# Another order of the x products of a step, and of VectorE's first operations, in a one-core LSTM

## The chip, the cores and the metric

The kernel runs on one core of a Trainium2 chip. The metric is device time in microseconds from launch to end. The engines are named as in the profile: PE (TensorE, matmul; PEld its weight loads), DVE (VectorE), ACT (ScalarE), POOL (GpSimd) and SP (SyncE, which here only issues DMAs). Each engine runs its own queue in order; they meet through semaphores.

## The reference

An LSTM over 512 steps, batch 32, width 512, four gates, whose outputs are added to its input:

```
xW = einsum('ntd,dg->ntg', x, Wx) + b          # x: 32 x 512 x 512, Wx: 512 x 2048
def step((h, c), xw_t):
    a = xw_t + h @ Wh                          # Wh: 512 x 2048
    i, f, o = sigmoid(a[:, :512]), sigmoid(a[:, 512:1024]), sigmoid(a[:, 1024:1536])
    g = tanh(a[:, 1536:])
    c = f * c + i * g
    h = o * tanh(c)
    return (h, c), h
out = x + h over all steps                     # h starts as cond_1024, c as 0; float32
```

## The kernel before

**Two kinds of matmul share PE.** The h part (`h_part`, L667 to L678) of step k is h times Wh, 64 matmul instructions that add into PSUM banks which ACT has seeded with the x part (`seed_first`, `seed_last`). It needs the transposed h of the step before (`ht`, L706). The x part, x times Wx plus bias, depends on no h; it is worked out ahead, in pieces which stand on PE between the h part of one step and that of the next, while the cell (`cell`: ACT L694 to L696 and L700, DVE L697 to L706) turns gates into the next h.

**The x part by fewer products.** The first four steps, the next four and the last sixteen are multiplied directly (`direct`, L604; L620 adds the bias). All others go through two layers of sums. The outer layer takes 24 steps of x (three rows of eight; a "block" below) by 20 products of sums of x blocks ("nodes", DVE L348) with sums of Wx blocks; each of the 20 is a *job*. The inner layer takes a job by seven products, numbered 1 to 7, from four "x sums" of the node (DVE L376 to L379) and differences of the weights (DVE L211 to L213, tiles t; factors made of several blocks are made once by `push_factors`, stored in DRAM, and reloaded for each job into the rings wa and wb). Steps 8 to 39 (the head) use the inner layer alone, two factors for each product; this is also where the first jobs lie.

**The windows of a job.** A job has a window w; window v goes with step k = v - 4. `products(v)` (L422 to L429) issues, from several jobs at once: product 1 of job v, product 6 of job v - 1, product 7 of job v - 2, products 2 and 3 of job v - 3, product 4 of job v - 4; product 5 in the job's own window or the next. Five of six windows start a job. Products 1, 6 and 7 add up in one half of a bank `acc`; 5 goes into `p5` (p in the trace), 2, 3 and 4 into two of three banks `pp`. A job's half of `acc` shares its bank with the half of the job two windows away.

**What is read in between.** `evacuate(v)` (L431 to L459), issued before `products(v)`, reads the running products: first, by a call with `FIRST_SUMS` as its room, due x sums and nodes; then `finish`, which reads the complete halves of `pp` (DVE L563 adds, ACT L551 copies); ACT's copy of `acc` after product 1 (L442) and of `p5` (L446); DVE's L449, acc plus p5 after product 6, ahead of product 7; more due sums (room `BETWEEN`); ACT L455 and L456, which seed the job's `pp`; and DVE's L457, acc plus p5 after product 7.

**What DVE does when.** `due` is a list sorted by window: x sums, nodes, sums of finished products (L579), factor sums. `run_due(v, room)` goes through it from the front. What is due by v is done; what is due later is done if it is ready and its columns plus 160 fit into the room left. An x sum is charged 128 + 160 = 288, a node 512 + 160 = 672, an L579 1024 + 160 = 1184. When the first call has done something, the whole of `FIRST_SUMS` is charged to the step's room of 3400.

**POOL and SP.** POOL adds the residual (L710) after each transposed h and the bias to the loaded x part (L652). SP issues, step by step, the loads of the x part (L649), of the rings (wa L771, wb L775) and of the rows, and the stores. Reloading a buffer of the ring wa waits for the last product that reads it, 6 or 5.

**The start** (L789 to L832) is written out by hand. On PE: 16 direct pieces into four banks, `products(0)`, then the direct parts of the steps 4 to 7, into the gate banks again, with `products(1)` to `products(3)` between them. On DVE: `t_sums(i)`, three differences each (L211 to L213), for the eight weight blocks; the first x sums (`prepare(0)`, L280 to L283, which need a loaded row); `keep_direct` (L620), which empties the four banks; then the factor sums (L248, L252).

Of the kernel before, what the change touches and what calls it, by code (L numbers as in the profile page):

```python
# [44 lines left out]
NODES = 8  # L45
FIXED = 160
ROOM = 3400
FIRST_SUMS = 600
BETWEEN = 1200
HEAD_ROOM = 5000  # L50
SLACK = [1, 1, 3]
# [55 lines left out]
def windows_of(k):  # L107

    return [k + 4]
# [17 lines left out]
def kernel(  # L127
# [49 lines left out]
    def load_residual(t):  # L177
        m = xr[t] = xr[t + 1] = opool.tile([P, 2, NJ, B], F32, name=f"xr_{t}", tag="xr")
        i, a = divmod(t, ROW)
        nc.sync.dma_start(  # L180
            out=m.rearrange("p t q b -> p (t q b)"),
            in_=x[i][:, a * P : (a + 2) * P],
        )
# [24 lines left out]
    def t_sums(i):  # L208
        w, t = raw[i], tt_[i]
        return [  # L210
            lambda: nc.vector.tensor_sub(t[:, 0:2], w[:, 1::2], w[:, 0:2]),  # L211
            lambda: nc.vector.tensor_sub(t[:, 2], w[:, 3], t[:, 0]),
            lambda: nc.vector.tensor_sub(t[:, 3], w[:, 2], t[:, 2]),  # L213
        ]
# [85 lines left out]
    def run_due(v, room):  # L300

        i = 0
        while i < len(due):
            window, _, columns, fn, ready = due[i]
            if window > v and (columns + FIXED > room or not ready(v)):
                i += 1
                continue
            assert ready(window)
            due.pop(i)
            fn()  # L310
            room -= columns + FIXED
            i = 0
# [88 lines left out]
    def product(job, s):  # L401
        dst = {
            1: job.acc,
            6: job.acc,
            7: job.acc,
            5: p5[:, 0],
            2: job.pp[0][:, 0],
            3: job.pp[0][:, 1],
            4: job.pp[1][:, 0],
        }[s]  # L410
        for m, (a, w) in enumerate(job.factors(s)):
            for t in range(4):
                nc.tensor.matmul(  # L413
                    dst[t * B : (t + 1) * B],
                    a[:, t],
                    w,
                    start=s in (1, 5) and m == 0,
                    stop=True,
                    skip_group_check=True,
                )  # L420

    def products(v):  # L422
        for late, ss in ((1, (6,)), (4, (4,)), (2, (7,)), (0, (1,)), (0, (5,)), (1, (5,)), (3, (2, 3))):
            job = jobs.get(v - late)
            for s in ss if job else ():
                if s != 5 or job.w5 == v:
                    product(job, s)
                if s == 4:
                    job.release()  # L429

    def evacuate(v, room):  # L431
        before = len(due)
        run_due(v - 0.5, FIRST_SUMS)
        taken = FIRST_SUMS if len(due) < before else 0
        for half, late in ((1, 5), (0, 4)):
# [160 lines left out]
    def flat(bank):  # L596
        return bank if len(bank.shape) == 2 else bank.rearrange("p n c -> p (n c)")

    def direct(t, bank, qs=range(4)):
        i, a = divmod(t, ROW)  # L600
        for q in qs:
            k, e = divmod(q, 2)
            for j in range(NJ):
                nc.tensor.matmul(  # L604
                    flat(bank)[j * B : (j + 1) * B],
                    rows[i][:, a, q],
                    raw[NJ * k + j][:, 2 * e : 2 * e + 2].rearrange("p n c -> p (n c)"),
                    start=q == 0,
                    stop=True,
                    skip_group_check=True,  # L610
                )

    def keep_direct(t, bank, room=None):
        if room is not None:
            xw[t] = room
        elif t < 4:
            xw[t] = upool.tile([P, G * P], F32, name=f"xw_{t}", tag="xw", bufs=4)
        else:
            xw[t] = node_free[t - 4].rearrange("p t e b -> p (t e b)")
        nc.vector.tensor_add(xw[t], flat(bank), bias_sb)  # L620
# [25 lines left out]
    def load_xw(t):  # L646
        xw[t] = upool.tile([P, G * P], F32, name=f"xw_{t}", tag="xw", bufs=4)
        i, a = divmod(t, ROW)
        nc.sync.dma_start(out=xw[t], in_=stored[i][a])  # L649

    def add_bias(t):
        nc.gpsimd.tensor_add(xw[t], xw[t], bias_sb)  # L652
# [3 lines left out]
    def seed_first(t):  # L656
        if t < T:
            nc.scalar.copy(gates[t % 2][:, 0:IFG], xw[t][:, 0:IFG])  # L658

    def seed_last(t):  # L660
        if t < T:
            nc.scalar.copy(gates[(t + 1) % 2][:, IFG:], xw[t][:, IFG:])
# [66 lines left out]
    def prepare(v):  # L729

        job = jobs.get(v)
        ops = []
        if job is None or job.w >= START:
            return ops
        i, j = job.kind
        for k in range(2):
            if (i, k) not in head_sums:
                if (i, 0) not in head_sums:
                    both = spool.tile([P, 2, 4, 4, B], F32, name=f"s_h{i}", tag="sums", bufs=2)
                head_sums[i, k], more = inner_sums(block(raw_block(i, k)), both[:, k])  # L740
                ops += more
        job.factors = lambda s: [
            (left(block(raw_block(i, k)), s, head_sums[i, k]), raw_factor(NJ * k + j, s)) for k in range(2)
        ]
        job.finish = finish_unit(job, i, j)
        job.release = lambda: None
        return ops
# [40 lines left out]
    with tc.manual_schedule():  # L788
        warm = work.tile([P, G, P], F32, name="warm", tag="s")  # L789
        nc.scalar.activation(warm[:, 0], c_init, AF.Sigmoid)  # L790
        for m in range(3 * NJ):
            nc.tensor.matmul(
                pps[2][m % NJ * B : (m % NJ + 1) * B].rearrange("p n c -> p (n c)"),
                c_init[:, 0:B],
                c_init.unsqueeze(1).to_broadcast([P, 4, P]),
                start=True,
                stop=True,
            )
        nc.vector.transpose(
            bias_sb.rearrange("p (m l) -> p m l", l=B),  # L800
            bias_t.unsqueeze(2).to_broadcast([P, G * NJ, B]),
        )
        firsts = [gates[0], gates[1], pps[0], pps[1]]
        for q in range(4):
            for t in range(4):
                direct(t, firsts[t], (q,))
        for i in range(5):
            for op in t_sums(i):
                op()
        for op in prepare(0):  # L810
            op()
        products(0)
        for i in range(5, 8):
            for op in t_sums(i):
                op()
        push_factors()
        for t in range(4):
            keep_direct(t, firsts[t])
        for v, t in enumerate(range(4, ROW), 1):
            direct(t, gates[t % 2])  # L820
            for op in prepare(v):
                op()
            if v < 4:
                evacuate(v, 0)
            run_due(0, 2400)
            keep_direct(t, gates[t % 2])
            if v < 4:
                products(v)
                fetch(v)
        seed_first(0)  # L830
        seed_last(0)
        seed_first(1)  # L832

        for k in range(T):
            if k % 2 == 0 and k + 2 < T:
                load_residual(k + 2)
            if 2 * 4 - 3 <= k and k + 3 < END:
                load_xw(k + 3)
            h_part(k)
            if 2 * 4 - 2 <= k and k + 2 < END:  # L840
                add_bias(k + 2)
            for m, v in enumerate(windows_of(k)):
                if v == START:
                    assert len(due) == 0 or due[0][0] >= START
                    free.extend(t.rearrange("p (h n) c -> p h (n c)", h=2) for t in others)
                    free.extend(spool.tile([P, 2, 2 * C], F32, name=f"slot_h{i}", tag="sums", bufs=2) for i in range(2))
                announce(v)
                room = ROOM if v >= START - 4 else HEAD_ROOM
                run_due(v, room - evacuate(v, room))
                products(v)  # L850
                tail_products(v)
                fetch(v)
                if k == T - 2:
                    x_last()
                if m == 0:
                    cell(k)
                    seed_first(k + 2)
                    seed_last(k + 1)
                for op in prepare(v + 1):
                    op()  # L860
        assert not due
# [51 lines left out]
```

## Time and profile before

| | |
|---|---|
| median of three runs | 3141.46 us (3139.4 to 3142.04) |
| profiled execution | 3141.61 us, span 3139.8 us |
| PE busy | 3113.1 us (99%), 56632 matmul instructions |
| DVE busy | 2248.2 us (72%) |
| ACT busy | 1615.8 us (51%) |
| POOL busy | 983.1 us (31%) |
| h part (L671) | 32704 instructions, mean 379 ns, in flight several at a time |
| one step inside the blocks | 6.04 us with six products, 5.61 us with five |

A row of a group or of the time line names start, duration, engine, line, operation, what is written and what is read, the shapes and a count; square brackets tell how long the engine was idle before it and who ended that. PE's busy time counts until the modelled end of a matmul, which reaches into the next one's time; so a wait of PE costs a little more than the idle time shown. A view by windows gives the length of a stretch, the busy time of each engine in it with its count of instructions, the granted share of PE's clock, the DMA share and the rate.

### The profile page before, as it was taken

The page shows a single profiled execution, that of the slowest core. Times are in us where ns is not written, and L with a number is a line of the kernel's source. Part 1 is how long each engine was busy: PE and PEld are TensorE (multiplying, and loading weights), DVE is VectorE, ACT ScalarE, POOL GpSimd, SP SyncE. Part 2 cuts the span into 40 slices and gives each one's busy share as a digit, 9 for nine tenths or more (in the row PEclk, how much of TensorE's full clock was granted, in tenths as well). Part 3 has the DMA queues.
Part 4 walks back from the last instruction along what each step waited for, and adds up shares of the span by engine and source line. Part 5 has one row for each costly group of instructions (what it writes and reads, how often), then busy time and mean ns, then how long its engine had stood idle before and what let it go on. Part 6 is the DMA issues. An engine that isn't in the chain of part 4 may idle for free.

```text
span 3139.8 us, 133260 instructions
## 1 busy us (share of the span) xinstructions
PE 3113.1 (99%) x56632; PEld 1797.3 (57%) x56632; DVE 2248.2 (72%) x6107; ACT 1615.8 (51%) x4842; POOL 983.1 (31%) x1001
## 2 busy tenths in 40 slices
PE   9999999999999999999999999999999999999999
PEld 4555665555555555566555555555556655655544
DVE  6547777777777777777777777777777777777533
ACT  2455555555555555555555555555555555555433
POOL 0123333333333333333333333333333333333320
PEclk9999999999999999999999999999999999999999
DMA  6656675766675766757666757667566667576510
GB/s 226 216 161 203 212 232 180 233 197 228 209 226 180 233 203 211 234 180 230 199 226 208 230 181 231 199 213 233 181 230 195 227 205 234 185 233 197 161 56 25
DMA packets 316083, 631.61 MB, mean 201 GB/s; under 512 B 41952, under 2 KB 107744, under 8 KB 314976
## 3 DMA queue, kind: packets, MB, share of 16 engines
q1 hardware_dynamic: 315344, 623.09, 61.4%
q8 instruction: 445, 7.29, 1.0%
q14 instruction: 150, 1.23, 0.1%
q10 hardware_dynamic: 144, 0.01, 0.0%
HBM read 448.60 MB, written 174.33 MB: 198 GB/s over the span
## 4 chain that ended last, share of the span: by engine, by line
PE 90%; DMA 4%; DVE 3%; issue 2%; SPq 1%; POOL 1%; ACT 0%; POOLq 0%; DVEq 0%
PE gates L671 51%; PE pp L413 16%; PE acc L413 16%; PE p L413 5%; DMA xw<-xw 3%; PE pp L604 1%; DVE node L348 1%; DVE slot L563 1%; PE acc L604 1%; PE gates L604 0%; POOL xw L652 0%; DMA row<-in_x_dram 0%; DVE s L376 0%; PE p L604 0%; POOL oc L710 0%
## 5 line engine op out<-in xcount | busy, mean ns | idle before, releaser
L671 PE MATMUL gates<-wh_sb,ht 128*32 128x384 f32 x32704 | 1861.1, 379 | 7.2 <-DVE ht L706 7.1
L671 PEld LDWEIGHTS gates<-wh_sb,ht 128*32 128x32 f32 x32704 | 1022.3, 110 | 877.9 <-issue 755.4
L710 POOL TENSOR_TENSOR oc<-xr,ht 128x128 f32<-128x128 f32 x509 | 357.2, 702 | 2010.6 <-DVE ht L706 1996.6
L652 POOL TENSOR_TENSOR xw<-xw,bias_sb 128x512 f32<-128x512 f32 x488 | 640.8, 1313 | 128.0 <-DMA xw<-xw 71.9
L694 ACT ACTIVATE s<-gates 128x256 f32<-128x256 f32 x512 | 196.3, 383 | 790.1 <-PE gates L671 790.1
L697 DVE TENSOR_TENSOR fc<-s,c 128x128 f32<-128x128 f32 x511 | 154.1, 302 | 376.4 <-ACT s L694 374.8
L455 ACT COPY pp<-pu 128x512 f32<-128x512 f32 x396 | 237.2, 599 | 107.8 <-DVE slot L563 56.0
L701 DVE TENSOR_TENSOR fc<-s,ig 128x128 f32<-128x128 f32 x512 | 150.9, 295 | 192.5 <-ACT ig L700 192.5
L696 ACT ACTIVATE s<-gates 128x128 f32<-128x128 f32 x512 | 141.9, 277 | 188.7 <-PE gates L671 188.7
L658 ACT COPY gates<-xw 128x384 f32<-128x384 f32 x492 | 232.6, 473 | 8.3 <-DVE node L620 4.6
L413 PE MATMUL pp<-wb,node 128*32 128x256 f32 x3040 | 235.0, 379 | 0.0
L457 DVE TENSOR_TENSOR pp<-acc,p 128x256 f32<-128x256 f32 x396 | 168.6, 426 | 63.1 <-ACT pp L456 63.1
L456 ACT COPY pp<-acc 128x256 f32<-128x256 f32 x396 | 142.3, 359 | 108.3 <-DVE slot L563 52.3
L706 DVE STREAM_TRANSPOSE ht<-fc 128x128 f32<-128x128 f32 x511 | 159.1, 311 | 53.4
L700 ACT ACTIVATE ig<-c 128x128 f32<-128x128 f32 x512 | 158.5, 310 | 75.1 <-DVE c L699 42.2
L442 ACT COPY pu<-acc 128x256 f32<-128x256 f32 x396 | 147.3, 372 | 71.9 <-PE acc L413 71.6
L449 DVE TENSOR_TENSOR pu<-acc,p 128x256 f32<-128x256 f32 x396 | 163.5, 413 | 23.9 <-ACT p L446 23.8
L413 PE MATMUL acc<-wa,s 128*32 128x256 f32 x2128 | 164.6, 379 | 0.0
L413 PE MATMUL pp<-wb,s 128*32 128x256 f32 x2128 | 164.5, 379 | 0.0
L413 PE MATMUL p<-wa,s 128*32 128x256 f32 x2128 | 164.5, 379 | 0.0
L413 PE MATMUL acc<-wb,s 128*32 128x256 f32 x2128 | 164.5, 379 | 0.0
L446 ACT COPY p<-p 128x256 f32<-128x256 f32 x396 | 149.6, 378 | 28.2 <-PE p L413 20.6
(187 smaller groups left out, 3964.7 us busy)
## 6 DMA issues: line engine op xcount, KB each, us to landing
wb<-keep_b SPq DMA_DIRECT2D x266, 512.0 KB, 5.4
xw<-xw SPq DMA_DIRECT2D x488, 256.0 KB, 4.1
wa<-keep_a SPq DMA_DIRECT2D x266, 384.0 KB, 4.6
xw<-slot SPq DMA_DIRECT2D x528, 128.0 KB, 3.2
xr<-in_x_dram SPq DMA_DIRECT2D x256, 128.0 KB, 3.3
out_dram<-oc SPq DMA_DIRECT2D x255, 128.0 KB, 2.9
row<-in_x_dram SPq DMA_DIRECT2D x63, 512.0 KB, 6.2
xw<-slot_h SPq DMA_DIRECT2D x180, 128.0 KB, 3.7
```

The costliest lines, as they stand in the source:

```text
L413: nc.tensor.matmul(dst[t * B : (t + 1) * B], a[:, t], w, start=s in (1, 5) and m == 0, stop=True, skip_group_check=True,)
L449: nc.vector.tensor_add(job.pu[:, 1], job.acc, job.p5)
L455: nc.scalar.copy(job.pp[0], job.pu)
L457: nc.vector.tensor_add(job.pp[1][:, 1], job.acc, job.p5)
L652: nc.gpsimd.tensor_add(xw[t], xw[t], bias_sb)
L658: nc.scalar.copy(gates[t % 2][:, 0:IFG], xw[t][:, 0:IFG])
L671: nc.tensor.matmul(g[j * B : (j + 1) * B, cols], state["ht"][:, k, :], wh_sb[:, k, j, cols], start=False, stop=True, skip_group_check=True,)
L694: nc.scalar.activation(s[:, 0:2], g[:, 0:2], AF.Sigmoid)
L697: nc.vector.tensor_mul(fc, s[:, 1], state["c"])
L700: nc.scalar.activation(tc_t, c, AF.Tanh)
L706: nc.vector.transpose(ht.rearrange("p q b -> p (q b)"), h)
L710: (nc.gpsimd if t < T - 3 else nc.vector).tensor_add(state["oc"][:, tt % 2], xr[t][:, tt % 2], ht)
```

## The change

Three things change. In `products`, product 6 of the job before moves from the first place to the fourth, behind 4, 7 and 1; these three move up by one place. `FIRST_SUMS`, the room of the x sums and nodes ahead of the reads of the products, grows from 600 to 1000, and so does what is charged for it. In the start, one more round of `t_sums` stands before the first x sums (six instead of five), and the four `keep_direct` stand behind `products(0)` and ahead of the last two rounds, not behind these. `push_factors` only fills the list.

```
-FIRST_SUMS = 600
+FIRST_SUMS = 1000
...
     def products(v):
-        for late, ss in ((1, (6,)), (4, (4,)), (2, (7,)), (0, (1,)), (0, (5,)), (1, (5,)), (3, (2, 3))):
+        for late, ss in ((4, (4,)), (2, (7,)), (0, (1,)), (1, (6,)), (0, (5,)), (1, (5,)), (3, (2, 3))):
...
-        for i in range(5):
+        for i in range(6):
             for op in t_sums(i):
                 op()
         for op in prepare(0):
             op()
         products(0)
-        for i in range(5, 8):
+        for t in range(4):
+            keep_direct(t, firsts[t])
+        for i in range(6, 8):
             for op in t_sums(i):
                 op()
         push_factors()
-        for t in range(4):
-            keep_direct(t, firsts[t])
```

## The prediction

> **What bounds the kernel now.** I read the page first, then who waited for whom on PE, then two places in order of time: the start, and one step that is longer than its neighbours. The profiled execution took 3141.61 us for a span of 3139.8 us (1.8 us lie around the span); the median of the runs is 3141.46 us, 0.15 us less. From the page (busy time; the chain that ended last, by engine):
>
> ```profile
> span 3139.8 us, 133260 instructions
> PE 3113.1 (99%) x56632; PEld 1797.3 (57%) x56632; DVE 2248.2 (72%) x6107; ACT 1615.8 (51%) x4842; POOL 983.1 (31%) x1001
> PE 90%; DMA 4%; DVE 3%; issue 2%; SPq 1%; POOL 1%; ACT 0%; POOLq 0%; DVEq 0%
> ```
>
> PE is the bound; no matmul is added or taken away, so all that can be won is time in which PE waits. Whom PE waited for (total us, times, longest):
>
> ```profile
> PE acc L413 <- DVE pp L457: 10.9, 20, 0.8
> PE gates L671 <- DVE ht L706: 7.1, 5, 1.7
> PE gates L604 <- DVE xw L620: 2.7, 1, 2.7
> ```
>
> Three waits. The first comes 20 times, the third once; the second lies in the tail, where no product covers the cell. One of the 20 places, first two steps side by side (length; PE busy; then PEld, DVE, ACT, POOL, clock, DMA), then PE, DVE and POOL in order of time:
>
> ```profile
> 1469.31:1475.35 6.04, 6.04 (x116) 4.02 (x112) 4.00 (x11) 4.03 (x13) 1.83 (x3) 1.00 0.98 339
> 1475.35:1482.37 7.02, 6.28 (x116) 3.66 (x112) 6.16 (x14) 2.79 (x9) 2.06 (x3) 1.00 0.37 149
> ```
>
> ```profile
> 1475.35 3.66 PE L671 MATMUL gates<-wh_sb,ht 128*32 128x384 f32 x64
> 1479.76 0.64 PE L413 MATMUL acc<-t,s 128*32 128x256 f32 x8 [0.74 <-DVE pp L457]
> ...
> 1482.37 3.64 PE L671 MATMUL gates<-wh_sb,ht 128*32 128x384 f32 x64
> 1485.83 0.61 PE L413 MATMUL acc<-wa,s 128*32 128x256 f32 x8
> ```
>
> ```profile
> 1476.95 0.42 DVE L449 TENSOR_TENSOR pu<-acc,p 128x256 f32<-128x256 f32 x1
> 1477.28 1.75 DVE L348 TENSOR_TENSOR node<-row,node 128x512 f32<-128x512 f32 x1
> 1479.07 0.29 DVE L376 TENSOR_TENSOR s<-node 128x128 f32<-128x128 f32 x1
> 1479.28 0.43 DVE L457 TENSOR_TENSOR pp<-acc,p 128x256 f32<-128x256 f32 x1
> 1479.61 0.28 DVE L697 TENSOR_TENSOR fc<-s,c 128x128 f32<-128x128 f32 x1
> ...
> 1481.19 0.31 DVE L706 STREAM_TRANSPOSE ht<-fc 128x128 f32<-128x128 f32 x1
> ```
>
> ```profile
> 1477.21 1.28 POOL L652 TENSOR_TENSOR xw<-xw,bias_sb 128x512 f32<-128x512 f32 x1 [2.20 <-DMA xw<-xw]
> ```
>
> The step is 7.02 us instead of 6.04. Product 6, first behind the h part, is held until L457 has read the neighbouring half of its accumulator's bank (1479.28 + 0.43 = 1479.71). In the next step the first product comes 1485.83 - 1482.37 = 3.46 us after the h part began; here that would be 1478.81, so the wait costs 0.95 us, of which the profile calls 0.74 idle: 0.21 is the pipelined end of the matmul before. Six products, five of them left out above, fill 1479.76 to 1482.37, 0.43 each. L457 is late because a node in front of it took 1.75 us, and that node ends (1479.03) 0.54 us after POOL's L652 (1477.21 + 1.28 = 1478.49). What a node takes (min/median/max, ns):
>
> ```profile
> L348 DVE TENSOR_TENSOR node<-row,node x114: 676/684/1767, 235.3 to 2918.4; 128x512 f32<-128x512 f32 x114
> ```
>
> The start, PE, then DVE, then the granted clock (the 7th figure) in two stretches:
>
> ```profile
> 21.44 1.07 PE L413 MATMUL p<-t,s_h 128*32 128x256 f32 x16
> 25.25 5.34 PE L604 MATMUL gates<-raw_sb,row 128*32 128x512 f32 x32 [2.74 <-DVE xw L620]
> ```
>
> ```profile
> 33.00 3.62 PE L604 MATMUL gates<-raw_sb,row 128*32 128x512 f32 x32
> ```
>
> ```profile
> 18.08 0.29 DVE L280 TENSOR_TENSOR s_h<-row 128x128 f32<-128x128 f32 x1 [0.88 <-DMA row<-in_x_dram]
> ...
> 19.95 0.69 DVE L211 TENSOR_TENSOR t<-raw_sb 128x512 f32<-128x512 f32 x1
> ...
> 24.52 1.28 DVE L620 TENSOR_TENSOR xw<-gates,bias_sb 128x512 f32<-128x512 f32 x2
> ```
>
> ```profile
> 26.70:28.90 2.20, 2.20 (x15) 0.47 (x11) 2.20 (x5) 0.00 (x0) 0.00 (x0) 0.50 0.53 204
> 28.90:30.40 1.50, 1.50 (x16) 0.44 (x12) 0.50 (x1) 0.00 (x0) 0.00 (x0) 0.84 0.02 8
> ```
>
> PE waits 2.74 us for the first L620, which stands on DVE behind three rounds of factor differences (19.95 to 24.52, 1.52 each). Then the clock is granted at 0.50 to 0.84 and 32 matmuls take 5.34 us instead of 3.62.
>
> **The change, part by part.**
>
> *Start on DVE.* One round of L211 to L213 moves from behind the head's x sums to before them: DVE is free at 18.08 - 0.88 = 17.20 and waits for a row, so 0.9 of its 1.52 us fill that gap. The eight sums (18.08 to 19.95, 1.87 us) end at 17.20 + 1.52 + 1.87 = 20.59. The first L620 then comes directly and ends near 21.3; PE asks for it at 21.44 + 0.86 = 22.30. So the 2.74 us go, 0.21 of pipelined end with them, and, with no idle PE, the half clock: 5.34 - 3.62 = 1.72. Together 4.67 us. Late next would be L620 of the fifth step: the rounds 6 and 7 (3.04 us) and four L620 (2.4 us) now end near 26, the factor operations behind them as now; PE needs that bank only two steps of about 6 us further on. Bounds: 2.74 (the slow clock has another cause) to 4.67; I take 4.67, the row being directly behind the wait.
>
> [...] The trace shows the half clock behind exactly this gap.
>
> *Product 6 behind 4, 7 and 1.* Product 4 goes into a bank that nothing in this step's evacuation touches. 7 needs L449 (ended 1477.37; 7 would start at 1478.81 + 0.43 = 1479.24) and the third x sum; 1 needs its node (ended 1479.03; wanted 1479.67). 6 would start at 1478.81 + 3 x 0.43 = 1480.10, and L457 ended at 1479.71: no wait, even with DVE unchanged. The 20 waits cost 10.9 us idle plus 20 x 0.21 of pipelined ends, 15.1; 20 times the longest, 16.0, is the upper bound, 10.9 the lower; I take 15.1, worked out as in the place shown. What is late next is the cell behind the same L457: h was ready at 1481.50 plus a hop to PE, and PE would be free at 1482.37 - 0.95 = 1481.42. The hop:
>
> ```profile
> 2940.36 0.31 DVE L706 STREAM_TRANSPOSE ht<-fc 128x128 f32<-128x128 f32 x1
> ```
>
> ```profile
> 2940.82 3.66 PE L671 MATMUL gates<-wh_sb,ht 128*32 128x384 f32 x64 [0.95 <-DVE ht L706]
> ```
>
> 2940.82 - 2940.67 = 0.15, so 0.23 us come back in this place; the mean place (10.9 / 20 = 0.55 idle, 0.2 less than here) gives 0.03. Over 19 or 20 places 0 to 4.6; I take 1.9. Moved with 6: the reload of the ring wa on SP waits for 6 and stands ahead of wb, rows and xw; it is issued up to 1.29 us later, but for a product two steps (12 us) on, so I take nothing. ACT reads none of it in that step.
>
> *FIRST_SUMS 600 to 1000.* A sum is charged 288, a node 672: three sums, or a node and a sum, now fit ahead of the reads of the products, where two sums fitted. Nothing is added. What moves up falls away before L457, so L457 and the cell stay or come earlier; L449 comes later by at most 0.68 + 0.29 less the idle time it fills. 7's margin of 1479.24 - 1477.37 = 1.87 us covers that. Worth: 0 to 1.9 (it can remove the returned cell time); loss bounded by the last rival. I take 0.
>
> Sum: 3141.61 - 4.67 - 15.1 + 1.9 = 3123.7 us; the runs' median stands 0.15 us below the profiled time, so **3123.6 us**.
>
> **The rivals.**
>
> *Half comes back* (7 or the cell waits in the same places for half the time): 3141.5 - 4.7 - 7.5 = 3129.3. For it: DVE was busy 6.16 of 7.02 us there, with another step of such load behind. Against it: 7's margin.
>
> *Only the start counts*: the whole block wait returns behind another operation, so that the reorder does nothing: 3136.8. For it: L457 holds the cell as well as 6. Against it: h was ready only 0.08 + 0.15 us too late in that step.
>
> *Slower: nodes collide with POOL.* Nodes move to just behind the transpose of h, where POOL adds the residual and the bias. A step with five products has the least cover:
>
> ```profile
> 1392.04 3.66 PE L671 MATMUL gates<-wh_sb,ht 128*32 128x384 f32 x64
> ...
> 1397.65 0.81 PE L671 MATMUL gates<-wh_sb,ht 128*32 128x384 f32 x5
> ```
>
> ```profile
> 1395.30 0.29 DVE L697 TENSOR_TENSOR fc<-s,c 128x128 f32<-128x128 f32 x1 [0.48 <-ACT s L694]
> ...
> 1396.90 0.31 DVE L706 STREAM_TRANSPOSE ht<-fc 128x128 f32<-128x128 f32 x1
> ```
>
> Its h is ready at 1397.21 + 0.15, 0.29 us before PE is free, and DVE idles 0.48 ahead of the cell: 0.77 us of cover. A node moved in front (0.68) and held by POOL as the longest was (1767 - 684 ns = 1.08) adds 1.76, so PE would wait 0.99 us: 18.8 us over 19 blocks of 24 steps. One such step in each block takes the gain back (3142.4), two end at 3123.6 + 37.6 = 3161.2. Against it: where a 1024-column sum is due the room is used up and no node moves; the other steps are 6.04 us long; a node that moves up leaves its old place.
>
> [...]
>
> **How the numbers follow.** Forecast 0.68 (own range 3120.5 to 3127: none to all of the cell time back, the start's clock either way), half back 0.12, only the start (or one collision in each block) 0.10, slower 0.10. A measurement of this kernel can tell about 0.2% (6.3 us) from no change. Faster therefore 0.68 + 0.12 = 0.80, same 0.10, slower 0.10. Lower end: 3141.5 - 4.67 - 16.0 = 3120.8, rounded down to 3120.5; the upper end takes in the half case and a little of the next: 3136.
>
> **What would show it.** Right: no PE wait on L620 near 22 us, no clock of 0.50 between 22 and 31 us; the wait of acc on L457 gone from PE's list; the long step of each block at 6.0 to 6.3 us. Wrong: a new row on PE behind L449, an x sum or the transpose of h with 19 or 38 entries; more nodes or sums over 1 us; h waits in the five-product steps.

## The result, and the profile after

The changed kernel takes 3123.49 us (median, 3122.18 to 3124.46) against 3140.89 us for the kernel before (3139.4 to 3142.04), six executions each: a ratio of 0.9944, 95% interval 0.9932 to 0.9957. It is 17.4 us faster; the prediction was 3123.6. The profiled execution took 3124.46 us for a span of 3122.6 us, so the two spans differ by 17.2 us.

The page of the kernel after, the same three lines as were shown of before:

```profile
span 3122.6 us, 133354 instructions
PE 3108.1 (100%) x56632; PEld 2022.5 (65%) x56632; DVE 2253.4 (72%) x6107; ACT 1606.1 (51%) x4842; POOL 1068.6 (34%) x1001
PE 99%; DVE 0%; ACT 0%; DMA 0%; issue 0%; SPq 0%; DVEq 0%
```

The same 56632 matmuls, and the chain that ended last now runs on PE for 99% of its length instead of 90%. Whom PE waited for (total us, times, longest):

```profile
PE gates L671 <- DVE ht L706: 7.8, 7, 2.6
PE gates L604 <- DMA raw_sb<-in_L_cond_Wx_dram: 1.5, 1, 1.5
PE pp L792 <- DVE c_init L194: 1.1, 1, 1.1
```

Two of the three rows of before are gone: the 20 waits of acc on L457, and the wait for L620 at the start. The third, for h, has grown from 5 waits to 7 and from a longest of 1.7 us to 2.6. In the stretch from 200 to 2800 us, which holds nearly all blocks, PE's busy time (second figure) before:

```profile
200.00:2800.00 2600.00, 2590.33 (x47916) 1518.40 (x47912) 1971.61 (x5330) 1400.11 (x4184) 871.25 (x866) 1.00 0.66 212
```

and after:

```profile
200.00:2800.00 2600.00, 2599.57 (x48157) 1723.49 (x48153) 1983.73 (x5359) 1398.96 (x4208) 955.30 (x870) 1.00 0.66 213
```

PE was idle for 9.67 us of 2600 before and for 0.43 after. Next to nothing is left to win there by taking away waits; what PE still loses lies at the two ends.

**The start.** PE, then DVE, then the stretch that had the half clock (the 7th figure is the granted clock):

```profile
21.27 1.07 PE L413 MATMUL p<-t,s_h 128*32 128x256 f32 x16
22.13 3.64 PE L604 MATMUL gates<-raw_sb,row 128*32 128x512 f32 x32
```

```profile
20.32 1.28 DVE L620 TENSOR_TENSOR xw<-gates,bias_sb 128x512 f32<-128x512 f32 x2
...
28.16 0.68 DVE L620 TENSOR_TENSOR node<-gates,bias_sb 128x512 f32<-128x512 f32 x1
```

```profile
26.70:28.90 2.20, 2.20 (x40) 1.36 (x36) 2.20 (x5) 0.74 (x2) 0.00 (x0) 1.00 0.53 203
```

The first L620 begins at 20.32 us instead of 24.52. PE goes from the head's product to the fifth direct group without a gap (21.27 to 22.13, 0.86 us), and the 32 matmuls take 3.64 us instead of 5.34, at clock 1.00 where it was 0.50.

**The long step.** The same step as shown of before: PE, DVE and POOL in order of time:

```profile
1464.75 3.66 PE L671 MATMUL gates<-wh_sb,ht 128*32 128x384 f32 x64
1468.20 0.64 PE L413 MATMUL pp<-wb,node 128*32 128x256 f32 x8
1468.63 0.64 PE L413 MATMUL acc<-wb,s 128*32 128x256 f32 x8
1469.06 0.64 PE L413 MATMUL acc<-wa,node 128*32 128x256 f32 x8
1469.49 0.64 PE L413 MATMUL acc<-t,s 128*32 128x256 f32 x8
...
1470.79 0.53 PE L671 MATMUL gates<-wh_sb,ht 128*32 128x384 f32 x4
```

```profile
1463.80 0.65 DVE L348 TENSOR_TENSOR node<-row,node 128x512 f32<-128x512 f32 x1
...
1466.68 1.04 DVE L379 TENSOR_TENSOR s<-row,s 128x128 f32<-128x128 f32 x1
...
1467.85 0.42 DVE L457 TENSOR_TENSOR pp<-acc,p 128x256 f32<-128x256 f32 x1
```

```profile
1465.77 1.80 POOL L652 TENSOR_TENSOR xw<-xw,bias_sb 128x512 f32<-128x512 f32 x1 [1.00 <-DMA xw<-xw]
```

The step takes 1470.79 - 1464.75 = 6.04 us instead of 7.02. Products 4, 7, 1 and 6 stand in the new order. L457 ends at 1468.27 and product 6 begins at 1469.49: 1.2 us to spare. The other eighteen long steps of before take 6.04 us too. Both edits are seen here: with the old order 6 would stand first, at 1468.20, and would still be 0.07 us too early. The node has moved up to just behind the transpose of h, clear of POOL's L652, and what meets L652 now is an x sum of L379, 1.04 us instead of its usual 0.28. Over the whole run, L348 with row and node (min/median/max, ns), and L379 with a row:

```profile
L348 DVE TENSOR_TENSOR node<-row,node x114: 647/650/682, 227.0 to 2897.4; 128x512 f32<-128x512 f32 x114
L379 DVE TENSOR_TENSOR s<-row,s x114: 247/278/1401, 202.0 to 2912.2; 128x128 f32<-128x128 f32 x114
```

No node of that form is held any more (the longest was 1.77 us). X sums are held more often: what all 380 of L379 took beyond their median adds up to 35 us, against 19 before.

**The end of the blocks.** From 2930 us on there is a step with no product behind its h part. PE, the cell's L699 on DVE, POOL, and the granted clock in the h part that follows:

```profile
2926.42 3.66 PE L671 MATMUL gates<-wh_sb,ht 128*32 128x384 f32 x64 [1.22 <-DVE ht L706]
2932.68 5.16 PE L671 MATMUL gates<-wh_sb,ht 128*32 128x384 f32 x64 [2.59 <-DVE ht L706]
```

```profile
2930.21 1.24 DVE L699 TENSOR_TENSOR c<-fc,ig 128x128 f32<-128x128 f32 x1
```

```profile
2930.03 1.27 POOL L652 TENSOR_TENSOR xw<-xw,bias_sb 128x512 f32<-128x512 f32 x1 [3.21 <-DMA xw<-xw]
```

```profile
2932.70:2936.30 3.60, 3.60 (x28) 1.36 (x32) 0.00 (x0) 0.00 (x0) 1.63 (x2) 0.58 0.44 140
```

L652, let go by its DMA, meets L699, which takes 1.24 us. Nothing covers the cell here, so PE idles for 2.59 us, the clock falls (0.58 on average over this stretch), and the next h part takes 5.16 us instead of 3.66. The same h part before, and the L652 ahead of it:

```profile
2951.44 3.66 PE L671 MATMUL gates<-wh_sb,ht 128*32 128x384 f32 x64 [1.65 <-DVE ht L706]
```

```profile
2947.67 1.28 POOL L652 TENSOR_TENSOR xw<-xw,bias_sb 128x512 f32<-128x512 f32 x1 [1.15 <-DMA xw<-xw]
```

There L652 began 1.54 us after the h part of its step (2946.13) and was through before the cell; after, it begins 3.61 us behind it (2930.03 - 2926.42). Why the load that lets it go lands later was not followed. In all, such steps cost 2.46 us less before.

**The ledger.** For each group of four matmuls I took the distance from its start to the next group's start and subtracted the usual one for its size (the median of all such groups); what is left is time PE lost. It was 38.4 us before and is 21.1 us after, 17.2 less, as the spans say:

| where | before | after | difference |
|---|---|---|---|
| wait for L620 and the slow clock behind it | 4.67 | 0 | -4.67 |
| first product of a step's x part, 20 places | 15.3 | 0.15 | -15.1 |
| short waits for h behind the products | 1.6 | 1.9 | +0.3 |
| h behind a step without products | 8.1 | 10.5 | +2.46 |
| first direct groups and their DMA | 3.2 | 3.05 | -0.2 |
| the rest | 5.5 | 5.5 | 0 |

### The profile page after: what moved, and what is told of

It is laid out like the page before. It is cut to its first block, busy times and chain, and to the rows that moved or that the text cites. A ratio compares the mean times of both kernels' runs of the same rounds, so it can differ in the third digit from the quotient of the medians.

```text
span 3122.6 us, 133354 instructions
## 1 busy us (share of the span) xinstructions
PE 3108.1 (100%) x56632; PEld 2022.5 (65%) x56632; DVE 2253.4 (72%) x6107; ACT 1606.1 (51%) x4842; POOL 1068.6 (34%) x1001
## 4 chain that ended last, share of the span: by engine, by line
PE 99%; DVE 0%; ACT 0%; DMA 0%; issue 0%; SPq 0%; DVEq 0%
PE gates L671 57%; PE acc L413 17%; PE pp L413 17%; PE p L413 6%; PE pp L604 1%; PE gates L604 1%; PE acc L604 1%; PE p L604 0%; DMA raw_sb<-in_L_cond_Wx_dram 0%; DVE ig L698 0%; DVE c L699 0%; ACT s L694 0%; ACT ig L700 0%; DVE fc L701 0%; DVE fc L697 0%
## 5 line engine op out<-in xcount | busy, mean ns | idle before, releaser
L671 PEld LDWEIGHTS gates<-wh_sb,ht 128*32 128x32 f32 x32704 | 1131.9, 110 | 770.9 <-issue 667.2
L710 POOL TENSOR_TENSOR oc<-xr,ht 128x128 f32<-128x128 f32 x509 | 445.2, 875 | 1925.3 <-DVE ht L706 1908.2
L652 POOL TENSOR_TENSOR xw<-xw,bias_sb 128x512 f32<-128x512 f32 x488 | 638.3, 1308 | 110.6 <-DMA xw<-xw 66.6
L413 PE MATMUL pp<-wb,node 128*32 128x256 f32 x3040 | 243.9, 379 | 0.0
L700 ACT ACTIVATE ig<-c 128x128 f32<-128x128 f32 x512 | 158.7, 310 | 64.5 <-DVE c L699 31.8
L457 DVE TENSOR_TENSOR pp<-acc,p 128x256 f32<-128x256 f32 x396 | 167.7, 423 | 32.8 <-ACT pp L456 31.0
L413 PE MATMUL pp<-wb,s 128*32 128x256 f32 x2128 | 170.8, 379 | 0.0
L699 DVE TENSOR_TENSOR c<-fc,ig 128x128 f32<-128x128 f32 x512 | 151.5, 296 | 17.8
```

Of the source, the lines that this page charges most:

```text
L413: nc.tensor.matmul(dst[t * B : (t + 1) * B], a[:, t], w, start=s in (1, 5) and m == 0, stop=True, skip_group_check=True,)
L457: nc.vector.tensor_add(job.pp[1][:, 1], job.acc, job.p5)
L671: nc.tensor.matmul(g[j * B : (j + 1) * B, cols], state["ht"][:, k, :], wh_sb[:, k, j, cols], start=False, stop=True, skip_group_check=True,)
L700: nc.scalar.activation(tc_t, c, AF.Tanh)
L710: (nc.gpsimd if t < T - 3 else nc.vector).tensor_add(state["oc"][:, tt % 2], xr[t][:, tt % 2], ht)
```

## The experiments

The question was which edit is worth what, whether POOL's bias addition is what makes L457 late and the shared bank what makes 6 wait for it, and what the loss at the end comes from. The theory is the prediction's; the rivals are that the start's clock has another cause, that the room is what removes the waits, and that nodes moved forward collide with POOL.

**Only the new order of the products.**

```
-        for late, ss in ((1, (6,)), (4, (4,)), (2, (7,)), (0, (1,)), (0, (5,)), ...
+        for late, ss in ((4, (4,)), (2, (7,)), (0, (1,)), (1, (6,)), (0, (5,)), ...
```

> The kernel before with the new order of products alone. Theory (product 6, as the first behind the h part, waits for L457; three products in front of it cover that): the row of acc waiting for L457 goes from PE's list, 14.7 us are won, and the cell that is late behind the same L457 gives about 1.5 us of it back as waits for the transpose of h (from the start of L697 in the long step of each block, 3.67 to 4.26 us after the h part): 3140.9 - 14.7 + 1.5 = 3127.7 us. Rival (the wait moves to 7, 1 or the cell in full): 3140 to 3141 us with a new row of about 19 waits on PE. The start is as before: PE waits 2.7 us for L620.

Measured: 3130.02 us against 3141.33 us, ratio 0.9961 (0.9948 to 0.9975). PE's waits, two of the rows:

```profile
PE gates L671 <- DVE ht L706: 7.5, 6, 1.9
PE gates L604 <- DVE xw L620: 2.9, 1, 2.9
```

No row of L457 is left, so the order alone takes its wait away. But h behind the products now loses 3.89 us in 16 places, where the ledger of before has 1.58 in 4: 2.3 us of cell time come back, and the gain is 11.3 us, about 2 us short of what was expected.

**Only the room for x sums, 1000.**

```
-FIRST_SUMS = 600
+FIRST_SUMS = 1000
```

> The kernel before with FIRST_SUMS 1000 alone; 6 stays first. Theory (the sums and the node that stood in front of L457 move up, so L457 comes earlier): the waits of acc for L457 shrink but stay, in the long step and the one behind it; with L457 where the changed kernel has it they add up to about 9 us of the 14.7: 3135 us. Rival (the order is all, the room does nothing): 3141 us and the list of waits unchanged. Other rival (a node that moves up meets POOL): over 3145 us, with waits for the transpose of h.

Measured: 3136.61 us, ratio 0.9985 (0.9976 to 0.9993).

```profile
PE gates L671 <- DVE ht L706: 7.9, 7, 2.7
PE gates L604 <- DVE xw L620: 2.9, 1, 2.9
PE acc L413 <- DVE pp L457: 2.2, 7, 0.6
```

By idle time the room removes most of the same wait: 10.9 us in 20 places become 2.2 in 7. Counted by the starts of the matmuls, as in the ledger, it removes only about half: the first product still comes late in some 40 places, about 8 us in all where it was 15, close to the 9 us expected (the time is 1.6 us over the 3135 expected). The room also brings the longer wait for h at the end (2.7 us) by itself. So the order and the room win the same time; the order alone wins all of it, the room alone half.

**Only the start.**

```
-        for i in range(5):
+        for i in range(6):
             for op in t_sums(i):
                 op()
 ...
         products(0)
-        for i in range(5, 8):
+        for t in range(4):
+            keep_direct(t, firsts[t])
+        for i in range(6, 8):
             for op in t_sums(i):
                 op()
         push_factors()
-        for t in range(4):
-            keep_direct(t, firsts[t])
```

> The kernel before with the new start of VectorE alone. Theory (wait for L620 and the half clock behind it): 3140.9 - 4.7 = 3136.2 us, no granted clock of 0.50 near 27 us; the list of waits on L457 as before, 20 times. Rival (the half clock has another cause and stays): 3137.9 us.

Measured: 3137.08 us, ratio 0.9988 (0.9979 to 0.9996). PE's waits, then the stretch that was slow:

```profile
PE acc L413 <- DVE pp L457: 11.0, 20, 0.8
```

```profile
26.70:28.90 2.20, 2.20 (x40) 1.37 (x36) 2.20 (x5) 0.74 (x2) 0.00 (x0) 1.00 0.50 194
```

The time lies between the theory's 3136.2 and the rival's 3137.9 and doesn't decide between them; the trace does. The 20 waits stand as they were, and the clock at 26.7 to 28.9 us is 1.00 where it was 0.50. Only the order of DVE's work was touched and with it PE's gap, so without the gap this slow clock is gone. A gap of that length is not always followed by one (see "The slow clock" below).

**Order and start, without the room** (the kernel after, with the old number).

```
-FIRST_SUMS = 1000
+FIRST_SUMS = 600
```

> The changed kernel with FIRST_SUMS back at 600. Theory (order and start add up; the room is worth no more than the cell time that comes back): 3127.7 - 4.7 = 3123.0 us, within 2 us of the changed kernel, with short waits for the transpose of h in the long steps that the changed kernel has not. Rival (the room carries a good part of the gain): over 3127 us.

Measured: 3124.81 us, ratio 0.9944 (0.9932 to 0.9957).

```profile
PE gates L671 <- DVE ht L706: 7.6, 6, 2.0
```

The longest of these waits, at the end, in PE's order of time:

```profile
2935.03 3.66 PE L671 MATMUL gates<-wh_sb,ht 128*32 128x384 f32 x64 [1.96 <-DVE ht L706]
```

The time is 1.8 us over the expectation and 1.3 us above the kernel after, and the intervals overlap: by the times alone the room's worth in the presence of the order isn't settled. The two traces say what it does. Without room, h behind the products loses 4.53 us in 17 places, with it 1.9; but without room the end loses 8.4 us and with it 10.5. The room gives about 2.6 us in the blocks and takes about 2.1 at the end.

**Before, without POOL's bias addition.**

```
-            if 2 * 4 - 2 <= k and k + 2 < END:
-                add_bias(k + 2)
```

> The kernel before without POOL's L652 in the blocks: the bias of steps 8 to 495 is left out, everything else stays. Theory (L457 is late in the long step because a node ahead of it waits until POOL's L652 is through): without L652 that node takes 0.7 us instead of up to 1.75, L457 ends about 1 us earlier, before product 6 asks for it, and the 14.7 us of waits on L457 go without any new order: 3141.3 - 14.7 = 3126.6 us; no node over 1 us except by L710. Rival (VectorE has simply too much to do ahead of L457 in that step): 3138 to 3141 us, the row of waits stays at some 20.

Measured: 3125.58 us against 3140.04, ratio 0.9955 (0.994 to 0.997). PE's wait, and the nodes:

```profile
PE acc L413 <- DVE pp L457: 0.5, 1, 0.5
```

```profile
L348 DVE TENSOR_TENSOR node<-row,node x114: 675/682/686, 233.7 to 2902.9; 128x512 f32<-128x512 f32 x114
```

With L652 gone no node of this form takes over 0.69 us (the longest was 1.77), and of 20 waits one is left, in the old order. It is POOL's addition that made the node long and L457 late.

**Before, with 6 and L457 in different banks.** Successive windows of the residual then share a bank, instead of every second one; the sums aren't the reference's, and only its time is read.

```
-    job.acc = accs[w % 2][:, w // 2 % 2]
+    job.acc = accs[w // 2 % 2][:, w % 2]
```

> The kernel before, with the halves of the accumulator banks given out otherwise: two successive windows share a bank, not windows two apart. (Product 1 of a job then opens its half while its neighbour's sum in the same bank is still open, so that x part is not the reference's.) Theory (6 is held because L457 reads the other half of the bank that 6 writes): in the long step 6 and L457 now use different banks, the wait moves to product 7, third in the row and 0.86 us later, and shrinks from 0.3 to 0.95 us to under 0.1: 3141.3 - 14.7 + 1.5 of cell time = about 3128 us. Rival (6 waits for L457 for another reason, the order of VectorE's queue or the x sums): 3141 us and 20 waits as before.

Measured: 3132.86 us, ratio 0.9977 (0.9968 to 0.9986): 5 us slower than expected. The long step, PE and DVE in order of time, and PE's wait for h:

```profile
1469.86 3.66 PE L671 MATMUL gates<-wh_sb,ht 128*32 128x384 f32 x64
1473.32 0.64 PE L413 MATMUL acc<-t,s 128*32 128x256 f32 x8
```

```profile
1471.80 1.49 DVE L348 TENSOR_TENSOR node<-row,node 128x512 f32<-128x512 f32 x1
1473.32 0.29 DVE L376 TENSOR_TENSOR s<-node 128x128 f32<-128x128 f32 x1
1473.53 0.42 DVE L457 TENSOR_TENSOR pp<-acc,p 128x256 f32<-128x256 f32 x1
```

```profile
PE gates L671 <- DVE ht L706: 8.9, 9, 2.2
```

and the longest of these waits, PE in order of time:

```profile
2941.01 5.36 PE L671 MATMUL gates<-wh_sb,ht 128*32 128x384 f32 x64 [2.20 <-DVE ht L706]
```

The node is held as before (1.49 us), L457 is late as before, and 6 begins at 1473.32, 3.46 us after the h part and 0.63 us before L457 ends. So what 6 had waited for was the bank, not the data. The expectation missed what came back: h behind the products loses 4.23 us (1.58 before), the first product of other steps 2.53 us in 17 places, which did not wait before, and the end 10.3 us (8.1).

**After, with the last bias additions on DVE.** From step 475 on L652 is issued on DVE, behind the transpose of h, so that POOL has nothing there to collide with.

```
+LAST_POOL = END - 21
...
-            if 2 * 4 - 2 <= k and k + 2 < END:
+            if 2 * 4 - 2 <= k and k + 2 < END and k < LAST_POOL:
                 add_bias(k + 2)
...
+                    if LAST_POOL <= k and k + 2 < END:
+                        nc.vector.tensor_add(xw[k + 2], xw[k + 2], bias_sb)
```

> The changed kernel with the last bias additions (from step 475 on) on VectorE behind the transpose of h, not on POOL. Theory (in the one step without any product the cell's L699 meets L652 and takes 1.24 instead of 0.29 us, PE idles 2.59 us and runs the next h part at half clock, 5.16 us instead of 3.66): both go, 3123.5 - 2.4 = 3121.1 us, the h part after it at 3.66 us. Rival (the seeds, now behind VectorE's addition, come later and hold the h part): 3124 to 3127 us.

Measured: 3121.51 us, ratio 0.994 (0.9928 to 0.9953), the fastest of all. The same place at the end (line numbers are one higher), PE and DVE:

```profile
2931.46 3.66 PE L672 MATMUL gates<-wh_sb,ht 128*32 128x384 f32 x64 [1.65 <-DVE ht L707]
```

```profile
2929.94 0.29 DVE L700 TENSOR_TENSOR c<-fc,ig 128x128 f32<-128x128 f32 x1
```

L699 (here L700) takes 0.29 us instead of 1.24, PE waits 1.65 instead of 2.59, and the h part behind it is back at 3.66 us. The span is 2.7 us shorter than that of the kernel after (3119.9 against 3122.6). That settles the cause of the loss at the end; that this kernel as a whole is faster than the kernel after rests on the two traces, since the intervals of the two ratios overlap.

**After, with still more room, 1400.**

```
-FIRST_SUMS = 1000
+FIRST_SUMS = 1400
```

> The changed kernel with FIRST_SUMS 1400: two nodes, or a 1024-column sum that is not yet due, fit ahead of the reads. Theory (PE waits for nothing in the blocks, what moves up is covered): 3122 to 3125 us. Rival (what stands behind the transpose of h meets POOL and delays the reads and the cell beyond the 0.77 to 0.87 us of cover): over 3130 us, with waits for the transpose of h or for L457 in many steps.

Measured: 3123.43 us, ratio 0.9947 (0.9934 to 0.9959), the same as with 1000.

```profile
PE gates L671 <- DVE ht L706: 7.5, 5, 2.6
```

No wait is added, and the long one at the end stays. Moving more forward neither wins nor loses anything that these runs can tell.

**After, with L652 issued twice.** This asks how much cover the blocks have against POOL. The bias of the steps 8 to 495 is added twice, so the output isn't the reference's.

```
         nc.gpsimd.tensor_add(xw[t], xw[t], bias_sb)
+        nc.gpsimd.tensor_add(xw[t], xw[t], bias_sb)
```

> [...] Theory (the blocks are covered by 0.77 to 0.87 us only, and one more collision of 1.1 us in each of a few steps is beyond that): waits for the transpose of h come back in several steps of each block, 19 blocks x 2 to 4 steps x 0.3 to 0.5 us = 11 to 38 us: 3135 to 3162 us. Rival (the waiting operation of VectorE gets in between two operations of POOL, and the load simply spreads): under 3130 us.

Measured: 3179.16 us against 3141.54, ratio 1.0117 (1.01 to 1.0133). PE's waits (lines one higher):

```profile
PE gates L672 <- DVE ht L707: 35.4, 75, 3.3
...
PE acc L413 <- DVE pp L457: 0.8, 2, 0.5
```

The direction was as expected, the size beyond it (3135 to 3162). PE's wait for h comes 75 times instead of 7, 35.4 us of idle time instead of 7.8, and the kernel is now 37.6 us slower than the kernel before: the change's gain is lost three times over. The reordered product still hardly waits for L457 (twice): what breaks first under POOL's load is the cell.

## Why the prediction was right

**Start on DVE (-4.67).** Right in each part for the profiled execution. The first L620 was put at 20.59 and began at 20.32; the wait of 2.74 us, the pipelined end of 0.21 and the slow clock of 1.72 are gone, 4.67 us in the ledger. The two last rounds and the four L620 were put to end near 26 and ended at 25.83; L620 of the fifth step followed the factor operations at 28.16 and cost nothing, since PE needs its bank later still, as was said. The start alone measured -4.25 us, by medians.

**The slow clock.** The prediction put the slow clock down to the gap, which the trace shows right ahead of it (2.74 us of idle PE, then 0.50), and kept another cause as the lower bound of that part. For the profiled executions it took the better side: with the gap gone the clock at the start is 1.00 (26.7 to 28.9 us), in the kernel after and with the start's edit alone. But the length of the gap doesn't settle it. With only the room changed PE waits longer at the same place, and the 32 matmuls behind it keep the full clock:

```profile
25.20 3.64 PE L604 MATMUL gates<-raw_sb,row 128*32 128x512 f32 x32 [2.88 <-DVE xw L620]
```

With POOL's addition taken out PE waits 2.9 us there, and the mean granted clock of that execution is 1.000 (0.999 before). What may differ is how the gap lies to the times at which the clock changes: in the traces of before and after that happens only at whole multiples of 3.41 us from the start of its record (worked out in the last section). Before, most of the gap lay in one piece of that length:

```profile
22.54:25.95 3.41, 0.70 (x8) 0.29 (x12) 3.31 (x8) 0.37 (x1) 0.00 (x0) 1.00 1.02 423
25.95:29.37 3.42, 3.42 (x20) 0.87 (x16) 3.42 (x6) 0.00 (x0) 0.00 (x0) 0.50 0.57 216
```

PE is busy for 0.70 of 3.41 us, and the next piece runs at 0.50. How the longer gaps of the two other kernels lie to such pieces is not shown. So the 1.72 us are there to be won only in executions that have the slow piece, and that the profiled one had it was luck. Of 21 timed executions of the kernel before (the row that the first four experiments are compared with), 11 have a mean granted clock of 0.999 and a median of 3141.83 us, 10 have 1.000 and 3140.23 us. The pieces lie otherwise in each of the two traces (the record starts at 5.47 us before, at 3.71 after), and PE need not be idle for a whole one: in the kernel after it was busy for 1.16 of 3.41 us ahead of the slow piece at the end.

**Product 6 behind 4, 7 and 1 (-15.1).** Right in place, size and cause. The ledger has -15.1; the order alone removes all of it, without the collision it doesn't arise (POOL's addition taken out), and in another bank the late L457 doesn't hold 6. Worked out from one place plus 20 pipelined ends of 0.21, the term came out to a tenth; the idle time that the profile shows, 10.9, would have been 4 us too little. The upper bound of 16.0 was not of the same kind: it left the pipelined ends out.

**Cell time back (+1.9), and FIRST_SUMS (0).** These two were mis-sized, and their errors cancel in part. The 1.9 was picked from 0 to 4.6, not worked out. With the new order but without room 2.3 us (alone) and 2.95 us (with the start) came back, more than the 1.9. With room only 0.3 is left. So FIRST_SUMS was not worth 0 in the blocks but about 2.6 us, above the end of its range (0 to 1.9), because the cell time that it could remove had been put too low. The reason given was right: what moves ahead falls away before L457 and the cell. What the prediction did not see is that it also takes the node out of L652's way.

**What was not in the sum: +2.46 at the end.** The step that failed is "loss bounded by the last rival": that rival was priced for nodes in the five-product steps, at 0.99 us each, and it never happened there. The collision came in the step without products, where not a node but the cell's own L699 was held, and where a wait of 2.59 us brings the slow clock on top. (That part, 1.5 us, is again not in every execution: four of the six of the kernel after have a mean clock of 0.999 and take 3123.29 to 3124.46 us, two have 1.000 and take 3122.2.) The prediction had named the tail as the place "where no product covers the cell" and then left it out. The terms now make 3141.61 - 4.67 - 15.1 + 0.3 + 2.46 - 0.2 = 3124.4, against 3124.46 for the profiled execution; the sum given, 3123.7, was close because 1.6 us too much cell time stood against 2.46 us that were missing.

**The rivals.** "Half comes back" and "only the start counts" fell: the margin of 7 and of L457 held, 1.2 us in the step shown. "Slower" fell at the load that the kernel has, but its mechanism is real: with L652 doubled PE waits 75 times for h and the time is 3179 us. The collisions shown here are a node at 1.49 to 1.75 us instead of 0.68, an x sum at 1.04 instead of 0.28, and L699 at 1.24 instead of 0.29. The node of 1.75 us, the x sum and L699 were held for 1.07, 0.76 and 0.95 us, about the rest of the L652 beside them (1.21, 0.89 and 1.09 us); what counts is only what waits behind them.

**What was to be seen.** All three signs named came: no clock of 0.50 near 22 to 31 us, no row of L457, the long step of each block at 6.04 us (6.0 to 6.3). Of the signs against, more x sums over 1 us appeared, and cost nothing in the step shown; of the five-product steps inside the blocks only one waits for h, for 0.09 us.

## What to carry to other kernels

A wait can be removed at any of its links: here the same 15 us went by putting other work in front of the waiting product or by taking the collision away, and about half of them by moving the held operation out of the colliding engine's way; edits at two links of one chain don't add (11.3 + 4.7 + 4.25 us singly, 17.4 together). When DVE's order is changed, look where each of POOL's operations lands afterwards, and first of all in the steps that have no matmuls to cover the cell. To size a wait on PE, count by the starts of the matmuls, not by the idle time shown, and look at the clock in the stretch behind it, in more than one execution.

## What was not expected of the hardware

Whether a short gap on PE is followed by a slow clock is not settled by its length. In the traces of before and after the granted clock changes only at whole multiples of 3.4133 us from the start of its record. Before, it is full for 20.48 us (5.47 to 25.95, six times 3.4133), 0.50 for 3.41 us (25.95 to 29.37), and full again for 3109.54 us (to 3138.91, 911 times); after, full for 2928.63 us (3.71 to 2932.34, 858 times), 0.50 for 3.41 us (2932.34 to 2935.75), and full for 187.73 us (to 3123.49, 55 times). I laid pieces of this length over both traces, up to PE's last matmul, and took PE's busy time in every one. In the piece ahead of the slow one it was 0.70 us before and 1.16 us after. In all others that end before PE's last matmul does, it was 1.76 us or more (after, 3113.25 to 3116.66), and behind each of them the clock was 1.00. That a gap must empty most of one piece to bring the slow clock is my estimate from these two traces; they show nothing between 1.16 and 1.76 us.

Over the runs, the clock fell behind idle times of 2.74 us (before: 32 matmuls in 5.34 us instead of 3.64), 2.9 us (only the order: 0.50 at 26.7 to 28.9 us), 2.59 us (after: an h part in 5.16 instead of 3.66) and even 2.20 us (other banks: 5.36 instead of 3.66), and not behind 2.88 us (only the room: 3.64), nor behind 1.96 us (order and start: 3.66, clock 1.00). One slow piece cost 1.5 to 1.7 us.

Doubling L652 cost far more than expected: 55.7 us over the kernel after, in which PE was idle for only 0.43 us between 200 and 2800 us. DVE's busy time rose from 2253.4 to 2549.9 us, time in which its operations were held included. It may be that each step has a fixed cover, up to which a collision is free and past which it is paid in full; that is not shown: the runs have the two ends of it and not the point between.
